# Routed FFN: norms, logits and choice made in the block endings of the attention ahead of it, and its lists in source order

## The chip, the core and the metric

The kernel runs on one core of one Trainium2 chip. TensorE (PE; its weight loads are PEld) multiplies matrices, VectorE (DVE) and ScalarE (ACT) work elementwise, GpSimd (POOL) issues the indirect DMAs, SyncE (SP) the plain ones. Each engine takes its instructions in order; semaphores order them against each other. The metric is the device time of one execution in microseconds (us), of which the median of several runs is taken. Lower is better.

## What is computed

The input is 6250 rows of 256 numbers, a graph of 206250 edges sorted by destination, and a second edge list of 131072 edges. Four layers each add to the rows `x`:

```
x = x + gnn0(layernorm(x))    # graph attention, 4 heads of 64
x = x + ffn0(layernorm(x))    # 8 experts, 2 for each row
x = x + gnn1(layernorm(x))    # weighted sum over edges, two products
x = x + ffn1(layernorm(x))    # graph attention as router, 4 experts
```

The change lies between the first two. `ffn0` is

```
logits = xt @ Wr + br                      # xt = layernorm(x)
probs  = softmax(logits); the 2 greatest of 8, divided by their sum, are the gates
for each expert e:  h = gelu(layernorm(xt) * ln_g[e] + ln_b[e] @ W1[e] + b1[e])
out    = sum over the chosen e of gate * (h @ W2[e] + b2[e])
```

(in the third line the norm with its scale and shift is taken first, then the product). So each row is normed twice: `xt` feeds the logits, its own norm feeds the experts.

## The kernel before

Rows lie in SBUF as `X`, 49 blocks of 128 rows. `fast` (L1778) runs these stages in turn.

**First attention** (`gat_stream`, L1146, called at L1863). The sorted edges are 1612 tiles of 128, taken in 202 pieces of eight. The loop over `s_` (L1352) is a software pipeline under `tc.manual_schedule()`, so each engine gets its instructions in the order of the source: step `s_` gathers piece `s_` from the table `tab` (POOL, L1214), loads what piece `s_+2` needs (SP), scores piece `s_-2` (`node_parts`, `scores`), every fourth step finds the greatest scores of a batch of 32 tiles and takes their exponentials (`turn_scores`, `greatest`, `turn_back`, whose ACT and DVE lines are L1285 and L1286), builds the one-hot matrices of piece `s_-6`, weights its messages (`messages`, L1293) and sums those of piece `s_-7` on PE (`sums`, L1316). A piece's tile `g` has nine buffers. The message weights `pe` lie in a PSUM tile of their own. When a block of 128 rows is complete, `done` (L1845) divides, adds the bias, applies relu and adds to `X[:, b, :]` (L1861).

**Front of the routed FFN** (`ffn0`, L652). For chunks of seven blocks it makes `xt`, the norm of `X` (`layernorm`, L247: bn_stats L252, bn_aggr L253, Sqrt on ACT L242, reciprocal L244, one tensor_scalar L256), then `xn`, the norm of `xt`, stores `xn` to the DRAM table `tab_x` (L671), transposes `xt` by PE, multiplies it with `wr` (L678) and adds `br` (L679). Then, for all 49 blocks at once, softmax, `top2` (the rank of each expert by pairwise comparison, L274 and L276) and gates.

**Lists** (first half of `routed_ffn`, L457). Expert parameters are gathered into `par` and stored as `par_d` (L478 to L483). A running count per expert gives every (row, choice) its place; 98 pairs of one-hot matrices `ro`, `qo` (L549, L551) and a product (L553) turn the places into the lists `gi` (which row to gather, L560) and `so` (where to put the result).

**Experts** (second half). 56 tiles of 256 places: SP loads the expert's weights by a register that it reads from `te`, POOL gathers `xg` from `tab_x`, PE transposes, multiplies (L601), ACT applies gelu, PE multiplies (L614), POOL scatters to `tab_y`. Then `X` gets the two results of each row (L632).

**What is drawn from `beside`.** `ffn0` takes a generator: `sorted_edges` (L1396) sorts the 131072 keys of the second edge list on chip (its compare stages are L1447 and L1448 on tile `A`; from the eleventh merge on it also transposes by PE), and `runs_of` (L1520) prepares lists for the third layer. Four steps of it are drawn after every expert tile:

```python
for _ in range(4):
    next(beside, None)
```

`ffn0` and `routed_ffn` are not under `tc.manual_schedule()`: a planner with a cost model orders their instructions, and it may set instructions of the generator well ahead of their place in the source, into gaps that it sees, also into the norms and the lists.

Of the kernel before, what the change touches and what calls it, by code (L numbers as in the profile page):

```python
# [20 lines left out]
F32 = mybir.dt.float32  # L21
# [50 lines left out]
def tile_kernel(ctx, tc, src_ins, out):  # L72
# [192 lines left out]

    def top2(pool, v, n_exp, nt=NT):

        rank = pool.tile([P, nt, n_exp], F32, name="rank")
        cmp = pool.tile([P, nt, n_exp], F32, name="cmp")
        nc.vector.memset(rank, 0.0)  # L270
        for j in range(n_exp):
            for a, b, op in ((0, j, OP.is_gt), (j + 1, n_exp, OP.is_ge)):
                if a < b:
                    nc.vector.tensor_tensor(cmp[:, :, a:b], v[:, :, j:j + 1].to_broadcast([P, nt, b - a]),  # L274
                                            v[:, :, a:b], op=op)
                    nc.vector.tensor_add(rank[:, :, a:b], rank[:, :, a:b], cmp[:, :, a:b])  # L276
        sel = pool.tile([P, nt, n_exp], F32, name="sel2")
        nc.vector.tensor_scalar(sel, rank, 1.5, None, op0=OP.is_lt)
        return sel

    def per_row(pool, op, a, n_exp, name):
        r = pool.tile([P, NT], F32, name=name)
        nc.vector.tensor_reduce(r, a, AX.X, op)
        return r[:, :, None].to_broadcast([P, NT, n_exp])

    def divide(pool, dst, a, by, n_exp, name):
        r = pool.tile([P, NT], F32, name=name)
        nc.vector.tensor_reduce(r, by, AX.X, OP.add)
        nc.vector.reciprocal(r, r)
        nc.vector.tensor_mul(dst, a, r[:, :, None].to_broadcast([P, NT, n_exp]))  # L290
# [166 lines left out]
    def routed_ffn(keep, tab_x, sel, gates, pre, beside):  # L457
# [12 lines left out]
        par_d = dram.tile([n_exp, P, NPAR], F32, name="par_d")  # L470
# [4 lines left out]
        with tc.tile_pool(name="rk", bufs=1) as p, tc.tile_pool(name="rkw", bufs=4) as wp, \  # L475
                tc.tile_pool(name="rk_ps", bufs=1, space=PSUM) as pp:
            par = p.tile([P, n_exp, NPAR], F32, name="par")
            with nc.allow_non_contiguous_dma(reason="biases along the partitions"):  # L478
                for o, n, v in ((0, FC, b1), (FC, KD, I[f"{pre}_ln_g"]), (FC + KD, KD, I[f"{pre}_ln_b"])):
                    pt = p.tile([P, n_exp, n], F32, name=f"par{o}")  # L480
                    nc.sync.dma_start(pt, v.rearrange("e (c p) -> p e c", p=P))
                    nc.vector.tensor_copy(par[:, :, o:o + n], pt)
                nc.sync.dma_start(par_d.rearrange("e p c -> p e c"), par)  # L483
# [168 lines left out]
    def ffn0(beside):  # L652

        E0 = I["L0_ffn_Wr"].shape[1]
        with tc.tile_pool(name="f0", bufs=1) as f0:
            gates = f0.tile([P, NT, E0], F32, name="gates")
            sel0 = f0.tile([P, NT, E0], F32, name="sel0")
            tab_x = dram.tile([NP, D], F32, name="tab_x")
            with tc.tile_pool(name="f0w", bufs=2) as lp, \
                    tc.tile_pool(name="f0_ps", bufs=2, space=PSUM) as pp:  # L660
                wr = lp.tile([P, KD, E0], F32, name="wr", bufs=1)
                nc.sync.dma_start(wr, I["L0_ffn_Wr"].rearrange("(k p) f -> p k f", p=P))
                br = lp.tile([P, E0], F32, name="br", bufs=1)
                nc.sync.dma_start(br, rows(I["L0_ffn_br"]))
                lo = lp.tile([P, NT, E0], F32, name="lo", bufs=1)
                for t0, n in chunks(NT, CH):
                    xt = lp.tile([P, CH, D], F32, name="xt")
                    layernorm(lp, xt, X[:, t0:t0 + n, :], n)
                    xn = lp.tile([P, CH, D], F32, name="xn")
                    layernorm(lp, xn, xt, n)  # L670
                    nc.sync.dma_start(tab_x[t0 * P:(t0 + n) * P].rearrange("(t p) d -> p t d", p=P),  # L671
                                      xn[:, :n])
                    for j in range(n):
                        xT = lp.tile([P, KD, P], F32, name="xT")
                        transposed(pp, xT, xt[:, j, :])
                        pr = pp.tile([P, E0], F32, name="pr")
                        for k in range(KD):
                            nc.tensor.matmul(pr, xT[:, k], wr[:, k], start=(k == 0), stop=(k == KD - 1))  # L678
                        nc.vector.tensor_add(lo[:, t0 + j, :], pr, br)  # L679
                nc.vector.tensor_sub(lo, lo, per_row(lp, OP.max, lo, E0, "mx"))  # L680
                nc.scalar.activation(lo, lo, AF.Exp)
                pb = lp.tile([P, NT, E0], F32, name="pb", bufs=1)
                divide(lp, pb, lo, lo, E0, "sm")
                sel = top2(lp, pb, E0)
                nc.vector.tensor_copy(sel0, sel)
                nc.vector.tensor_mul(pb, pb, sel)
                divide(lp, gates, pb, pb, E0, "sg")
            routed_ffn(f0, tab_x, sel0, gates, "L0_ffn", beside)
# [95 lines left out]
    def general():  # L784
        with ExitStack() as held1:
# [57 lines left out]
            ffn0(iter(()))  # L843
# [302 lines left out]
    def gat_stream(s, H, CD, si, il, dl, tab, NI, early, done, parts=1, beside=None):  # L1146
# [13 lines left out]
        with ExitStack() as st:  # L1160
            pool = lambda name, bufs, **k: st.enter_context(tc.tile_pool(name=f"{s.name}_{name}", bufs=bufs, **k))
            gp = pool("gs", 1)
            mp = pool("gw", 2)
            pp = pool("gp", 1, space=PSUM)
            nid = window_nodes(s, gp)
            NB = gp.tile([P, NT, 3, ND], BF, name="NB")
            nb_d = dram.tile([NP, 3 * ND], BF, name=f"{s.name}_nb") if s.group else None
            nbw, sums_of, ready, moved = {}, {}, [], []
            with tc.tile_pool(name="split", bufs=1) as sp:
                r = sp.tile([P, NT, ND], F32, name="r")  # L1170
                nc.vector.tensor_copy(NB[:, :, 0, :], NI)
                nc.vector.tensor_sub(r, NI, NB[:, :, 0, :])
                nc.vector.tensor_copy(NB[:, :, 1, :], r)
                nc.vector.tensor_sub(r, r, NB[:, :, 1, :])
                nc.vector.tensor_copy(NB[:, :, 2, :], r)
                if s.group:
                    nc.sync.dma_start(nb_d.rearrange("(t p) d -> p t d", p=P), NB.rearrange("p t s d -> p t (s d)"))
            ips = place_iota(pp)
# [96 lines left out]
            def turn_back(i, d, M):  # L1275
                pz = pp.tile([P, 3, P], F32, name="zt")
                nc.tensor.transpose(pz[:, 0], d, ident)
                nc.tensor.transpose(pz[:, 1], M[:, :P], ident)
                pb = pz[:, :2].rearrange("p k (t h) -> p k t h", h=H)
                pe = ps[i] = (pp if parts == 1 else gp).tile([P, B, H], F32, name="pe", bufs=1)  # L1280
                nc.scalar.activation(pe, pb[:, 0], AF.Exp)
                for q in range(i * PB, min((i + 1) * PB, npiece)):
                    t0, n = span(q)
                    o = t0 - i * B
                    nc.scalar.activation(piece[q][:, :n, DH:DH + H], pb[:, 0, o:o + n], AF.Exp)  # L1285
                    nc.vector.tensor_tensor(piece[q][:, :n, DH + H:], pb[:, 1, o:o + n],  # L1286
                                            il[:, t0:t0 + n, None].to_broadcast([P, n, H]), op=OP.mult)

            def messages(q):
# [3 lines left out]
                nc.vector.tensor_mul(gh, gh, ps[i][:, o:o + n, :, None].to_broadcast([P, n, H, CD]))  # L1293
# [30 lines left out]
            def keep_sums():  # L1324

                while ended:
                    i = ended.pop(0)
                    t = mp.tile([P, W], F32, name="kept", bufs=3)
                    nc.scalar.copy(t, acc.pop(i).rearrange("p s w -> p (s w)"))
                    moved.append((i, t))  # L1330
# [17 lines left out]
            with tc.manual_schedule():  # L1348
# [3 lines left out]
                for s_ in range(max(npiece + 7, PB * nbatch + 3) + 2):  # L1352
# [4 lines left out]
                    beside()  # L1357
                    k, q = s_ - 2, s_ - 7
# [21 lines left out]
                    if s.group:  # L1380
                        keep_sums()
                        while ready:
                            b = ready.pop(0)
                            done(b, sums_of.pop(b), items.pop(b), mp)
                    while ended:
                        b = ended.pop(0)
                        done(b, acc.pop(b), items.pop(b), mp)
# [390 lines left out]
    def fast(flag_s0, last_d, dl_d):  # L1778
# [7 lines left out]
        tab = dram.tile([NP, D + H0], F32, name="tab")  # L1786
        with tc.tile_pool(name="gat0f", bufs=1) as g0:
            si = g0.tile([P, C * P], I32, name="si")
            dl = g0.tile([P, C * P], F32, name="dl")
            il = g0.tile([P, C * P], F32, name="il")  # L1790
# [54 lines left out]
            def done(b, acc, hs, mp):  # L1845
# [15 lines left out]
                nc.vector.scalar_tensor_tensor(X[:, b, :], o, 0.0, X[:, b, :], op0=OP.max, op1=OP.add)  # L1861

            gat_stream(s0, H0, C0, si, il, dl, tab, NI, early, done)  # L1863


# [6 lines left out]
        with tc.tile_pool(name="sort", bufs=1) as sp, tc.tile_pool(name="sort_ps", bufs=1, space=PSUM) as pp:  # L1872
# [4 lines left out]
            ffn0(itertools.chain(sorted_edges(s1, sp, pp, si1, dl1, il1, flag1),  # L1877
                                 runs_of(s0, sp, pp, si_d, wab_d, dab_d)))
# [239 lines left out]
```

## Time and profile before

| | us |
|---|---|
| median of 10 runs | 6606.87 (6602.35 to 6609.58) |
| the profiled execution | 6605.38 |
| its span | 6603.6 |
| first gather of the attention | 174.3 |
| last row of `X` from the attention written | 2249.1 |
| norms and logits | 2249.1 to 2374 |
| choice | 2374.4 to 2395.2 |
| lists | 2395.2 to 2461.9 |
| first expert product | 2474.6 |
| last expert product | 3325 |
| combination into `X` | 3325 to 3395 |
| weighted sum of the third layer | 3436 to 5495 |

Times in the profile are from the start of the span. Line numbers (L1214) are those of the kernel before. A group's row gives line, engine, operation, tiles, shape and count, then busy us, mean ns of one, then the idle time of the engine just before them with what ended it. A row of the timeline gives start, length, engine and instruction.

### The profile page before, as it was taken

How to read it: one execution, taken by the hardware profiler on the slowest of the kernel's cores; microseconds unless marked ns; L12 is line 12 of the kernel's file. 1: busy time of each engine (PE TensorE's matmuls, PEld its weight loads, DVE VectorE, ACT ScalarE, POOL GpSimd, SP SyncE). 2: the span in 40 equal slices, each digit the busy share in tenths (PEclk: the TensorE clock that was granted, in tenths of full speed). 3: DMA queues.
4: the chain of work that ended last, by engine and by line, in shares of the span. 5: the costliest groups of instructions: out<-in, count | busy, mean ns of one | idle time of the engine just before them, and what ended most of it. 6: DMA issues, size and time to landing. Idle time of an engine off the chain costs nothing.

```text
span 6603.6 us, 62175 instructions
## 1 busy us (share of the span) xinstructions
PE 3866.5 (59%) x17463; PEld 2941.9 (45%) x17463; DVE 4398.5 (67%) x10540; ACT 1008.7 (15%) x2527; POOL 4095.6 (62%) x4320
## 2 busy tenths in 40 slices
PE   4466666666666659999913566666666667111111
PEld 3344444444444448888712344444444445111111
DVE  5455555555555683345267888888888883888888
ACT  2000000000000102222300122222222223000000
POOL 0777777777777302233217777777777775777774
PEclk9677777777777669999955777887888788555555
DMA  4555555555555216556553444444444443233332
GB/s 134 139 139 137 137 140 138 137 139 137 138 139 138 73 50 205 184 192 218 179 188 107 115 118 123 122 122 118 123 122 122 118 122 75 61 68 68 68 69 53
DMA packets 495558, 821.80 MB, mean 124 GB/s; under 512 B 142672, under 2 KB 314915, under 8 KB 495170
## 3 DMA queue, kind: packets, MB, share of 16 engines
q0 software_dynamic: 190880, 462.26, 26.8%
q1 hardware_dynamic: 291654, 343.79, 17.3%
q10 hardware_dynamic: 12668, 11.68, 0.6%
q8 instruction: 141, 2.31, 0.1%
q14 instruction: 215, 1.76, 0.1%
HBM read 743.27 MB, written 77.29 MB: 124 GB/s over the span
## 4 chain that ended last, share of the span: by engine, by line
POOL 33%; PE 17%; issue 17%; DVE 16%; DMA 15%; ACT 1%; ACTq 0%; DVEq 0%; SPq 0%; another core or an unknown queue 0%; POOLq 0%
POOL g L234 17%; POOL g L1214 16%; DMA g<-tab,si 7%; PE ph L601 5%; PE py L614 5%; DMA g<-tab_ef,si 3%; PE acc L1316 3%; DMA g<-tab_1f,si1s 2%; DVE X L1756 2%; DVE run L1921 2%; DVE g L1293 1%; DVE oh L1107 1%; PE ph L1830 1%; DVE ot L1224 1%; DVE z L1246 1%
## 5 line engine op out<-in xcount | busy, mean ns | idle before, releaser
L234 POOL DMA_INDIRECT g<-tab_ef,si x1616 | 1532.9, 949 | 602.6 <-issue 574.0
L1214 POOL DMA_INDIRECT g<-tab,si x1612 | 1538.9, 955 | 494.5 <-issue 411.6
L1921 DVE SCALAR_TENSOR_TENSOR run<-g,wab,run 128x256 f32<-128x256 f32 x2626 | 1263.9, 488 | 339.9 <-DMA g<-tab_ef,si 264.3
L1316 PE MATMUL acc<-g,oh 128*128 128x264 f32 x3224 | 1052.5, 492 | 336.2 <-DVE g L1293 331.1
L1316 PEld LDWEIGHTS acc<-g,oh 128*128 128x128 f32 x3224 | 780.4, 250 | 559.5 <-DVE g L1293 389.5
L1214 POOL DMA_INDIRECT g<-tab_1f,si1s x787 | 769.9, 978 | 251.6 <-issue 212.1
L2035 PE MATMUL acc<-run,oh 128*128 128x256 f32 x808 | 319.4, 535 | 708.7 <-DVE oh L1925 705.7
L2035 PEld LDWEIGHTS acc<-run,oh 128*128 128x128 f32 x808 | 199.3, 264 | 818.1 <-issue 442.0
L1246 DVE TENSOR_TENSOR z<-g,nd 128x32 f32<-128x32 f32 (+1 forms) x301 | 58.0, 193 | 707.2 <-DMA g<-tab,si 644.9
L1293 DVE TENSOR_TENSOR g<-g,pe 128x2048 f32<-128x2048 f32 (+2 forms) x301 | 487.1, 1618 | 0.0
L1657 PE MATMUL pf<-xt,w 128*128 128x512 f32 (+1 forms) x832 | 416.8, 636 | 102.7 <-ACT h L1662 95.9
L1668 PE MATMUL pf<-w,h 128*128 128x256 f32 x1568 | 405.4, 409 | 71.3 <-ACT y L1673 60.7
L1316 PE MATMUL acc<-s,oh 128*128 128x72 bf16 x1267 | 96.4, 251 | 594.4 <-DVE s L1298 594.4
L601 PE MATMUL ph<-xe,w 128*128 128x256 f32 x1792 | 405.6, 383 | 4.5 <-DVE xe L589 4.5
L614 PE MATMUL py<-w,h 128*128 128x256 f32 x1792 | 398.7, 380 | 0.0
L1668 PEld LDWEIGHTS pf<-w,h 128*128 128x128 f32 x1568 | 317.5, 207 | 132.6 <-ACT y L1673 68.4
L577 POOL DMA_INDIRECT xg<-tab_x,gi x112 | 123.4, 1102 | 402.6 <-PE pt L586 317.2
L601 PEld LDWEIGHTS ph<-xe,w 128*128 128x128 f32 x1792 | 341.7, 193 | 50.7 <-DVE xe L589 4.9
L1316 PEld LDWEIGHTS <-oh 128*128 128x128 bf16 x1267 | 89.9, 133 | 598.5 <-issue 495.5
L614 PEld LDWEIGHTS py<-w,h 128*128 128x128 f32 x1792 | 336.6, 191 | 43.1
L617 POOL DMA_INDIRECT tab_y<-y,so x112 | 119.0, 1062 | 276.1 <-DVE y L616 271.5
L1235 PEld LDWEIGHTS <-ot 128*128 128x128 bf16 x2879 | 116.0, 101 | 389.9 <-DVE ot L1224 347.6
(494 smaller groups left out, 5751.1 us busy)
## 6 DMA issues: line engine op xcount, KB each, us to landing
w<-in_L_ffn_W SPq DMA_DIRECT2D x112, 1024.0 KB
db<-s_d SPq DMA_DIRECT2D x299, 256.0 KB
g<-tab_ef,si POOLq DMA_INDIRECT x1616
g<-tab,si POOLq DMA_INDIRECT x1612
y_d<-y SPq DMA_DIRECT2D x196, 128.0 KB
yb<-y_d SPq DMA_DIRECT2D x49, 512.0 KB
g<-tab_1f,si1s POOLq DMA_INDIRECT x787
yy<-tab_y SPq DMA_DIRECT2D x7, 1792.0 KB
```

The costliest lines, as they stand in the source:

```text
L234: nc.gpsimd.indirect_dma_start(out=dst, out_offset=None, in_=table, in_offset=bass.IndirectOffsetOnAxis(ap=si[:, t:t + 1], axis=0))
L601: nc.tensor.matmul(ph, w1[:, k, f * P:(f + 1) * P], xe[:, k, :], start=(k == 0), stop=(k == KD - 1))
L614: nc.tensor.matmul(py, hs[f][:, i * P:(i + 1) * P], w2[:, f, :], start=(f == 0), stop=(f == FC - 1))
L1214: nc.gpsimd.indirect_dma_start(out=g[:, j, :DH + H], out_offset=None, in_=tab, in_offset=bass.IndirectOffsetOnAxis(ap=si[:, t0 + j:t0 + j ...
L1246: nc.vector.tensor_add(z[:, :n], g[:, :n, DH:DH + H], nd[:, :n, :H])
L1293: nc.vector.tensor_mul(gh, gh, ps[i][:, o:o + n, :, None].to_broadcast([P, n, H, CD]))
L1316: nc.tensor.matmul(acc[b].rearrange("p s w -> p (s w)"), oh[:, t - a], m_, start=(t == lo), stop=(t == hi))
L1657: nc.tensor.matmul(ph[:, :n], w1[:, e, k, f * P:(f + 1) * P], xts[g][:, k, :n], start=(k == 0), stop=(k == KD - 1))
L1668: nc.tensor.matmul(py[:, :D], hs[g, e, f][:, j * P:(j + 1) * P], w2[:, e, f, :], start=(f == 0), stop=(f == FC - 1))
L1756: nc.vector.scalar_tensor_tensor(X[:, b, :], v[:, e, :], gates[:, j, e:e + 1], X[:, b, :], op0=OP.mult, op1=OP.add)
L1921: nc.vector.scalar_tensor_tensor(at[:, i] if j < Q - 1 else r[i], g[:, j, :], w, at[:, i], op0=OP.mult, op1=OP.add)
L2035: nc.tensor.matmul(acc[i], oh[:, k], r[k], start=(q % 2 == 0 and k == 0), stop=(last and k == 1))
```

## The change

1. A class `Head` holds `lo` (logits), `sel`, `gates`, `wr`, `br`, `tab_x` and `par_d`. It is made before the attention and lives until the experts are done.
2. The attention's `done` ends with `spread` (bn_stats, bn_aggr, Sqrt) and returns a next step. `gat_stream` collects such steps with `follow` and runs each in the next round of its loop, between the loads and the scores: `normed` (norm of the block, statistics of the result), `twice` (two PE transposes, one ACT copy), `logits` (second norm, store of 128 rows to `tab_x`, product with `wr`, ACT copy). After blocks 21, 43 and 48 `chosen` follows: bias, softmax, ranks and gates for the blocks since the last one (22, 22, 5), one step of the generator `select` per round. The loop runs on until no step is left.
3. `expert_params` is drawn as the attention's `beside`: its three loads are issued in the first round, copies and store come 20 draws later (five draws a round).
4. The PSUM tile of `pe` is replaced by one tile `mix` of 512 columns: `pe` in the first 128, the transposes in the next 256, the logits in eight more.
5. To make room, `il` is bf16, `kept` has two buffers for three, and the split of node values `NB` lies in the short-lived pool `split`; the pools of the pipeline open after that pool has closed.
6. The list part of `routed_ffn` comes under `tc.manual_schedule()`: its instructions run in source order, and the planner puts none of the generator's among them. The experts' part is as before, with the same generator.

The core of the diff, and the new functions:

```diff
-    def routed_ffn(keep, tab_x, sel, gates, pre, beside):
+    def expert_params(p, par_d, pre):
+        b1, g, b = (I[f"{pre}_{s}"] for s in ("b1", "ln_g", "ln_b"))
...
+            for o, n, v in ((0, FC, b1), (FC, KD, g), (FC + KD, KD, b)):
+                pt = p.tile([P, n_exp, n], F32, name=f"par{o}")
+                nc.sync.dma_start(pt, v.rearrange("e (c p) -> p e c", p=P))
+                parts.append((o, n, pt))
+            for _ in range(20):
+                yield
+            for o, n, pt in parts:
+                nc.vector.tensor_copy(par[:, :, o:o + n], pt)
+            nc.sync.dma_start(par_d.rearrange("e p c -> p e c"), par)
+    def routed_ffn(keep, tab_x, sel, gates, par_d, pre, beside):
...
-                tc.tile_pool(name="rk_ps", bufs=1, space=PSUM) as pp:
+                tc.tile_pool(name="rk_ps", bufs=1, space=PSUM) as pp, tc.manual_schedule():
...
+    def select(pool, tag, lo, br, sel, gates, n, n_exp):
+        wide = [P, n, n_exp]
+        nc.vector.tensor_add(lo, lo, br[:, None, :].to_broadcast(wide))
+        nc.vector.tensor_sub(lo, lo, per_row(pool, OP.max, lo, n, n_exp, f"mx{tag}"))
+        nc.scalar.activation(lo, lo, AF.Exp)
+        yield
+        divide(pool, gates, lo, lo, n, n_exp, f"sm{tag}")
+        yield
+        yield from ranks(sel, lo, gates, n_exp)
+        nc.vector.tensor_scalar(sel, sel, 1.5, None, op0=OP.is_lt)
+        nc.vector.tensor_mul(gates, gates, sel)
+        divide(pool, gates, gates, gates, n, n_exp, f"sg{tag}")
...
-            mp = pool("gw", 2)
-            pp = pool("gp", 1, space=PSUM)
...
-            NB = gp.tile([P, NT, 3, ND], BF, name="NB")
...
             with tc.tile_pool(name="split", bufs=1) as sp:
+                NB = (sp if s.group else gp).tile([P, NT, 3, ND], BF, name="NB")
...
+            mp = pool("gw", 2)
+            pp = pool("gp", 1, space=PSUM)
...
-                pe = ps[i] = (pp if parts == 1 else gp).tile([P, B, H], F32, name="pe", bufs=1)
-                nc.scalar.activation(pe, pb[:, 0], AF.Exp)
+                if i == 0:
+                    ps[0] = gp.tile([P, B, H], F32, name="pe") if pe is None else pe
+                nc.scalar.activation(ps[0], pb[:, 0], AF.Exp)
...
-                for s_ in range(max(npiece + 7, PB * nbatch + 3) + 2):
+                last, s_, later = max(npiece + 7, PB * nbatch + 3) + 1, -1, []
...
+                while s_ < last or later:
+                    s_ += 1
...
                     beside()
+                    now, later[:] = list(later), []
+                    for f, a in now:
+                        follow(f(*a))
...
+                return normed, (b, mp) + spread(mp, X[:, b, :])
+            def spread(mp, x):
+                bs = mp.tile([P, 6], F32, name="bs", bufs=3)
+                nc.vector.bn_stats(bs, x)
+                mv = mp.tile([P, 2], F32, name="mv", bufs=6)
+                nc.vector.bn_aggr(mv, bs)
+                sd = mp.tile([P, 1], F32, name="sd", bufs=6)
+                nc.scalar.activation(sd, mv[:, 1:2], AF.Sqrt, bias=eps)
+                return mv, sd
+            def scaled(mp, xl, x, mv, sd):
+                rs = mp.tile([P, 1], F32, name="rs")
+                nc.vector.reciprocal(rs, sd)
+                nc.vector.tensor_scalar(xl, x, mv[:, 0:1], rs, op0=OP.subtract, op1=OP.mult)
+            def normed(b, mp, mv, sd):
+                xt = mp.tile([P, D], F32, name="xt", bufs=3)
+                scaled(mp, xt, X[:, b, :], mv, sd)
+                return twice, (b, mp, xt) + spread(mp, xt)
+            def twice(b, mp, xt, mv, sd):
+                pt = mix[:, P:P + D].rearrange("p (k e) -> p k e", k=KD)
+                for k in range(KD):
+                    nc.tensor.transpose(pt[:, k], xt[:, k * P:(k + 1) * P], ident)
+                xT = mp.tile([P, KD, P], F32, name="xT")
+                nc.scalar.copy(xT, pt)
+                return logits, (b, mp, xt, mv, sd, xT)
+            def logits(b, mp, xt, mv, sd, xT):
+                scaled(mp, xt, xt, mv, sd)
+                nc.sync.dma_start(head.tab_x[b * P:(b + 1) * P], xt)
+                head.logits(mix[:, P + D:P + D + E0], xT, b)
+                if b in ends:
+                    t0 = max([e + 1 for e in ends if e < b], default=0)
+                    return chosen, (head.select(hp, t0, b + 1 - t0),)
+            def chosen(parts):
+                for _ in parts:
+                    return chosen, (parts,)
+            ends = (NT // 2 - 3, NT - 6, NT - 1)
...
+                mix = xp.tile([P, 4 * P], F32, name="mix")
+                par = head.params(hp)
+                gat_stream(s0, H0, C0, si, il, dl, tab, NI, early, done, beside=lambda: next(par, True) is None,
+                           pe=mix[:, :P].rearrange("p (b h) -> p b h", h=H0))
...
-            ffn0(itertools.chain(sorted_edges(s1, sp, pp, si1, dl1, il1, flag1),
-                                 runs_of(s0, sp, pp, si_d, wab_d, dab_d)))
+            head.ffn(f0, itertools.chain(sorted_edges(s1, sp, pp, si1, dl1, il1, flag1),
+                                         runs_of(s0, sp, pp, si_d, wab_d, dab_d)))
+        chosen_by.close()
```

## The prediction

> **What bounds the kernel now.** I read the page's chain first, then busy time by stage, then the timeline around the stage that is changed.
>
> ```profile
> POOL g L234 17%; POOL g L1214 16%; DMA g<-tab,si 7%; PE ph L601 5%; PE py L614 5%; DMA g<-tab_ef,si 3%; PE acc L1316 3%; DMA g<-tab_1f,si1s 2%; DVE X L1756 2%; DVE run L1921 2%; DVE g L1293 1%; DVE oh L1107 1%; PE ph L1830 1%; DVE ot L1224 1%; DVE z L1246 1%
> ...
> L1214 POOL DMA_INDIRECT g<-tab,si x1612 | 1538.9, 955 | 494.5 <-issue 411.6
> ```
>
> The first attention is L1214: 1612 gathers on POOL, 0.955 us each and 0.30 us of issue between them, 2033 us from 174 to 2207. The list of waits has no POOL wait there over 0.3 us but one of 3.1: POOL never waits for a buffer. I matched gathers with the sums that free their buffers: from the end of the sums of a piece to the gather that takes its buffer nine pieces later at least 20.3 us pass, with a piece every 10.09 us. So this stage has room on every engine but POOL.
>
> ```profile
> 1400.00:2000.00 600.00, 387.40 (x1634) 287.36 (x1632) 346.29 (x619) 32.39 (x148) 454.86 (x477) 0.75 0.51 139
> 2000.00:2249.00 249.00, 159.70 (x673) 120.20 (x671) 148.37 (x264) 15.00 (x66) 156.94 (x166) 0.78 0.42 113
> 2249.00:2374.00 125.00, 66.97 (x294) 58.64 (x294) 101.53 (x408) 24.29 (x65) 4.69 (x55) 0.50 0.16 53
> 2374.00:2467.00 93.00, 44.56 (x200) 31.79 (x200) 85.65 (x310) 0.53 (x1) 3.62 (x7) 0.72 0.15 23
> 2467.00:2700.00 233.00, 226.66 (x1069) 197.94 (x1070) 69.96 (x129) 63.08 (x131) 67.47 (x65) 0.97 0.63 207
> ```
>
> Columns: stretch, length, busy us of PE, PEld, DVE, ACT, POOL, then granted clock, DMA share, GB/s. In the attention DVE is busy 58% and ACT 5%. From 2249 to 2467, norms and logits, then choice and lists, DVE is busy 86% and POOL next to nothing: a serial stretch on DVE. Then the experts, with PE full.
>
> ```profile
> 2248.64 0.43 DVE L1861 SCALAR_TENSOR_TENSOR X<-o,X 128x256 f32<-128x256 f32 x1
> ...
> 2374.39 0.55 DVE L283 TENSOR_REDUCE mx<-lo 128x49 f32<-128x392 f32 x1
> ...
> 2395.20 1.35 DVE L486 TENSOR_TENSOR_SCAN inc<-sel 128x49 f32<-128x49 f32 x8
> ...
> 2403.09 0.20 DVE L482 COPY par<-par 128x64 f32<-128x64 f32 x1 [5.23 <-DMA par<-in_L_ffn_b]
> ...
> 2461.67 0.21 DVE L560 TENSOR_SCALAR gi<-gi 128x112 int32<-128x112 int32 x1
> ...
> 2474.55 9.77 PE L601 MATMUL ph<-xe,w 128*128 128x256 f32 x32
> ```
>
> This is the ruler: last row of X at 2249.07; choice from 2374.4; lists 2395.20 to 2461.88; first expert product 12.7 us later. From X to gi: 212.8 us, all on the path.
>
> **The change, term by term.** The 212.8 us fall away; five terms take their place.
>
> (a) In the attention, per block, DVE gets two bn_stats, two aggregates, two reciprocals, two 128x256 tensor_scalars. The same four shapes run in the weighted sum: 0.427 (L1984), 0.182 (L1986), 0.155 (L1993), 0.41 (L1995, its least): 2.4 us. PE gets two transposes and four logit passes, 1.5 us at half clock; ACT two Sqrt, two copies and up to four table loads of 1.28; SP one 128 KB store. A block ends every 41 us; in that time DVE waits 13.2 us for gathers to land (644.9 us over 49 blocks), so 2.4 us of work and some 5 us of waits fit. The steps `normed`, `twice`, `logits` each come one iteration later than their inputs, so little queues behind them. The select of 22 blocks is 4 small instructions, about 1 us, an iteration. The weighted sum shows the cover holding: there the same chain runs beside 1604 gathers with DVE 82% busy, and POOL waits 0.3 us at a time. What remains is POOL's own time. The 44 gathers there that overlap an L1995 average 0.966 us against 0.946 without neighbours, and in the attention those beside an L1198 store to the queue 0.99: 98 x 0.02 + 49 x 0.04, some **3 us** (0 to 14; the latter if each of the 98 costs the 0.14 by which the slowest common gathers, 1.087, exceed 0.946).
>
> The new tile `mix` puts `pe`, the transposes and the logits into one PSUM tile. How such sharing behaves is seen at L1285 and L1286: ACT and DVE read different parts of one `zt` and strictly alternate, each idle 0.26 us until the other ends. So the transposes wait for the message product (2.28 us) of the iteration before. PE stands there with `node_parts` behind it, DVE's `nd` behind that; about 1.2 us twice per block, inside the 20.3 us.
>
> (b) The drain, 2207 to 2249, has no POOL cover; DVE, PE and ACT alternate. Into it fall the endings of blocks 46 and 47 (DVE 2.4 and 1.8 us, PE 1.5 and 0.55), three steps of the second select (3 us), and two table loads back to Exp (2.6): 11.9 us, of which a little lies in existing waits: **10 us** (4 if only the loads and half of PE's part show, 20 with six hand-overs at `mix` at 1.2 us on top).
>
> (c) Block 48 has everything bare: statistics 0.6, table load and Sqrt 1.6, reciprocal and scaling 0.6, statistics and Sqrt 0.9, copy, logits, copy 1.6, hand-overs 0.3; then the select of 5 blocks: 3 small DVE instructions, table load, Exp, 3 more, 2.5; 28 rank instructions at 0.16 (L274 and L276 of the last stage, 0.160 and 0.169), 4.6; the last five 0.85. That is **14 us** (9 with loads hidden and pairs overlapping, 20 with every hand-over at 0.26).
>
> ACT's loads have a rule against them. In this trace the instruction behind each ACT_TABLE_LOAD starts 0.01 us after its 1.28. The Trainium skill ("ScalarE: Activation LUTs", What ACT_TABLE_LOAD costs) adds a drain of about 1.38 us to each load. By that rule four loads on the path in (b) and (c) would make the sum 5.5 us longer; the trace disagrees.
>
> (d) Lists, now in source order without the sort: 66.7 us less 10 sort compares ahead of the ro/qo loop (0.62 each from start to start, 6.2), 0.5 for two behind it, 6.4 for the wait on `par` and its copies, is 53.6. Filling is lost too: dependents start some 0.04 us after their input ends, independents 0.09 before; 25 instructions x 0.13 = 3.3. **57 us** (53 to 63). The loop itself, 98 x 0.445 = 43.6 us, is untouched.
>
> (e) The experts start 12.7 us behind gi as before. The sort's start, 11.4 us of preparation and 51 compares, moves here: 46 us of DVE. Its first 55 stages take 81 us in all; a tile of 14.25 us leaves DVE over 12 free, so they end by tile 7; the next step, which needs PE, ran at 2690.6, tile 15. So PE should not see it. POOL's 4.7 us of iotas and memsets and 1 MB of keys come here too: **2 us** (0 to 8).
>
> The moves of `par`, `wr` and `br` to the start cost nothing beside nine free buffers: `par` took 8.3 us to land, and POOL has 90 us before it needs a buffer back. SP is held 7.4 us issuing `par`, with the loads of two pieces ahead behind it, again under 20.3.
>
> Sum: 212.8 - (3 + 10 + 14 + 57 + 2) = 126.8. The profiled execution took 6605.4 us (span 6603.6), giving 6478.6; the median of the runs is 1.5 us higher, so **6480 us**. With the terms' ends the case runs from 6460 to 6519, where all bad ends meet.
>
> **Rivals.**
>
> 1. The pools move: g, db and the rest now open behind the closed `split`, which also holds `NB`. If g takes NB's place, the first gather (174.28) waits until NB is stored (issued 176.11, read from 189.77): 15.5 us later, all of it on POOL: 6495. For: POOL is the bound. Against: db is asked for first and is larger (6 KB against 3.9), and a late db costs 1.5 us of a slack of 20. 12%.
>
> 2. DVE's scalings hold POOL off: 98 x 0.41 us, 0.76 of it on a gather in work, 31 us: 6511. Against: the 0.966 above. The Trainium skill ("SBUF — State Buffer", SBUF: two separate sides) states that POOL can't write DMA descriptors while DVE runs a two-port instruction. 6%.
>
> 3. The experts give the sort back: 46 us, if the stages run at their places, 4 a tile, and PE stands before the transposes of the sort. It does stand later: of 150 us from 3099 PE is busy 132.7. 6526. 7%.
>
> 4. **Slower**: the block endings make DVE, not POOL, the bound of the attention, through the shared `mix`. It decides where a block's added work and waits exceed 13.2 us plus 126.8/49 = 15.8. I count 7.4; if hand-overs cost a whole iteration's alternation, 18 us say, it is 6480 + 49 x (18 - 13.2) = 6715. The 20.3 us help only once. 8%, a quarter of that near no change.
>
> 5. More gain: the 17 us of PE stalls just named depend on where the planner puts the sort; without them 6463, with light ends under 6455. 5%.
>
> **Numbers.** The forecast has 62%. The range 6455 to 6532 takes in the forecast and rivals 1 to 3. About 0.2% is what a measurement of this kernel can tell from no change: faster 0.92, same 0.02, slower 0.06.
>
> **What the profile would show.** (a) L1214 near 0.957 us, a piece still every 10.1 us, last gather near 2210; a gap over 0.3 us would speak for rival 4, a first gather near 190 for rival 1. (b, c) Last X near 2262, the last gates near 2276. (d) No A<-A compare between the scans and gi; gi near 2333. (e) First expert product near 2346, its 56 tiles still ending some 850 us later. I am wrong if pieces take over 10.3 us or the experts' stage grows by tens of us.

## The result, and the profile after

The changed kernel takes 6493.1 us (median of 8 runs, 6488.3 to 6496.6) against 6606.8 for the kernel before (28 runs): ratio 0.983, 95% interval 0.982 to 0.984. The forecast was 6480, the gain 113.7 us for 126.8 forecast. The span of the profiled execution fell from 6603.6 to 6486.6 us, by 117.0; the execution profiled after lies 4.7 us under the median of its runs.

The ruler of the prediction, in the timeline of the kernel after (start, length, engine, line):

```profile
187.90 1.10 POOL L1260 DMA_INDIRECT g<-tab,si  x1 [14.50 <-DMA s_nb<-NB]
...
2272.93 0.42 DVE L1921 SCALAR_TENSOR_TENSOR X<-o,X 128x256 f32<-128x256 f32 x1
...
2285.35 0.25 DVE L515 TENSOR_TENSOR_SCAN inc<-sel 128x49 f32<-128x49 f32 x1
...
2355.23 0.21 DVE L589 TENSOR_SCALAR gi<-gi 128x112 int32<-128x112 int32 x1
...
2366.46 3.78 PE L630 MATMUL ph<-xe,w 128*128 128x256 f32 x8 [0.64 <-DVE xe L618]
```

From X's last row to `gi` there are now 82 us instead of 213. But the first gather starts 13.6 us later, held by a DMA, the store of `NB`. Cut at these marks, the two spans compare so:

| stretch | before | after | difference |
|---|---|---|---|
| start to first gather | 174.3 | 187.9 | +13.6 |
| first to last gather | 2033.0 | 2036.7 | +3.7 |
| last gather to last row of X | 41.8 | 48.7 | +6.9 |
| last row of X to `gi` | 212.8 | 82.1 | -130.7 |
| `gi` to first expert product | 12.7 | 11.0 | -1.6 |
| the experts' products | 849.0 | 841.1 | -7.8 |
| the rest | 3280.1 | 3279.0 | -1.0 |

The stages by window (columns as in the prediction's windows):

```profile
1400.00:2000.00 600.00, 365.35 (x1682) 282.96 (x1681) 378.49 (x741) 84.24 (x236) 455.21 (x475) 0.76 0.52 141
2000.00:2273.00 273.00, 175.86 (x773) 134.60 (x772) 182.41 (x375) 44.16 (x115) 170.61 (x178) 0.81 0.43 115
2273.00:2285.00 12.00, 1.68 (x6) 1.21 (x6) 8.42 (x49) 2.58 (x7) 1.53 (x4) 0.50 0.07 22
2285.00:2355.00 70.00, 44.57 (x200) 31.27 (x200) 68.97 (x272) 0.00 (x0) 3.72 (x54) 0.79 0.05 16
```

In 600 us of the attention DVE does 32 us more and ACT 52 more, and POOL's 455 stand unchanged: the work went beside the gathers. Two groups of the profile's page (the second is VectorE's first instruction on the gathered rows, so what it waits for is the gathers) say what it used up:

```profile
L1260 POOL DMA_INDIRECT g<-tab,si x1612 | 1545.5, 959 | 505.7 <-issue 426.0
...
L1292 DVE TENSOR_TENSOR z<-g,nd 128x32 f32<-128x32 f32 (+1 forms) x301 | 58.0, 193 | 477.7 <-DMA g<-tab,si 419.6
```

A gather takes 0.959 us for 0.955 before, and no gap between two of them is over 0.32 us. VectorE's wait for gathers to land fell from 644.9 to 419.6 us: 4.6 us a block are spent, some 8.5 are left.

Seven of the runs below (e5 to e10, e12) fell on chips on which the kernel before takes 7802 to 7897 us, for a reason that stays open, and in their profiles POOL waits up to 16.8 us between two gathers; it does not pace the attention there, so of these runs single instructions are read, and times only beside each other.

### The profile page after: what moved, and what is told of

Same layout as the page of the kernel before. It is cut to its first block, busy times and chain, and to the rows that moved or that the text cites. A ratio compares the mean times of both kernels' runs of the same rounds, so it can differ in the third digit from the quotient of the medians.

```text
span 6486.6 us, 62324 instructions
## 1 busy us (share of the span) xinstructions
PE 3787.6 (58%) x17463; PEld 2900.3 (45%) x17463; DVE 4446.4 (69%) x10655; ACT 1161.7 (18%) x2758; POOL 4102.8 (63%) x4320
## 4 chain that ended last, share of the span: by engine, by line
POOL 23%; PE 13%; issue 11%; DVE 11%; DMA 6%; ACT 0%; ACTq 0%; DVEq 0%; another core or an unknown queue 0%; POOLq 0%; SPq 0%
POOL g L234 18%; PE ph L630 6%; PE py L643 5%; POOL g L1260 5%; DMA g<-tab_ef,si 3%; DMA g<-tab_1f,si1s 2%; DVE X L1813 2%; DVE run L2028 2%; DVE oh L1152 1%; DMA yy<-tab_y 0%; DVE ot L1270 0%; DVE qo L580 0%; PE pf L1714 0%; DVE X L661 0%; PE pt L615 0%
## 5 line engine op out<-in xcount | busy, mean ns | idle before, releaser
L1260 POOL DMA_INDIRECT g<-tab,si x1612 | 1545.5, 959 | 505.7 <-issue 426.0
L1363 PE MATMUL acc<-g,oh 128*128 128x264 f32 x3224 | 995.8, 472 | 225.0 <-DVE g L1340 220.3
L1363 PEld LDWEIGHTS acc<-g,oh 128*128 128x128 f32 x3224 | 754.5, 240 | 412.7 <-DVE g L1340 250.3
L1340 DVE TENSOR_TENSOR g<-g,mix 128x2048 f32<-128x2048 f32 x202 | 457.6, 2265 | 0.0
L1292 DVE TENSOR_TENSOR z<-g,nd 128x32 f32<-128x32 f32 (+1 forms) x301 | 58.0, 193 | 477.7 <-DMA g<-tab,si 419.6
L633 ACT ACTIVATE h<-ph,pa 128x256 f32<-128x256 f32 x448 | 212.3, 474 | 437.6 <-PE ph L630 436.7
```

The source lines that it names most:

```text
L633: nc.scalar.activation(h, ph, AF.Gelu, bias=pa[:, f:f + 1])
L1260: nc.gpsimd.indirect_dma_start(out=g[:, j, :DH + H], out_offset=None, in_=tab, in_offset=bass.IndirectOffsetOnAxis(ap=si[:, t0 + j:t0 + j ...
L1340: nc.vector.tensor_mul(gh, gh, ps[0][:, o:o + n, :, None].to_broadcast([P, n, H, CD]))
L1363: nc.tensor.matmul(acc[b].rearrange("p s w -> p (s w)"), oh[:, t - a], m_, start=(t == lo), stop=(t == hi))
```

## The experiments

**e1, the pool's buffers wait tile by tile.** This asks what holds the first gather.

```diff
-            mp = pool("gw", 2)
+            mp = pool("gw", 2, reuse_waits="tile")
```

> The changed kernel, but the pipeline's pool waits tile by tile for the memory of the pool that closed ahead of it, not for the whole of it. Theory A (rival 1 of the prediction, by way of the pool and not of one buffer's place: the first gather waits for the store of NB): first gather back near 174.5 from 187.9, all that follows 13 us earlier, 6493 becomes 6480. Theory B (the late start comes from the new loads at the front or from the nodes' own store): first gather stays at 187 to 190, 6493.

Measured: 6484.9 us (6476.6 to 6490.9), ratio to before 0.9815 (0.9802 to 0.9828). Its timeline at the start:

```profile
173.22 0.59 POOL L1182 IOTA s_nid<- 128x1 f32 x5 [104.10 <-DMA tab<-tb]
...
174.26 1.10 POOL L1260 DMA_INDIRECT g<-tab,si  x1 [0.45 <-POOL s_nid L1182]
```

The gather no longer waits for the store, only for POOL's own iota, and starts where it did before. So it was the reuse of the closed pool's memory that held it, and g's first buffer did not itself lie on `NB`: with waits counted tile by tile it had nothing to wait for. (One later gather, at 187.55, waits 0.6 us more than the others, put to a DMA.) The medians give back 8.2 of the 13.6 us. In the two profiled executions the first gather gains all 13.6, and the experts' products, which the edit does not touch, take 4.1 us more.

**e2, the lists without the manual order.**

```diff
-                tc.tile_pool(name="rk_ps", bufs=1, space=PSUM) as pp, tc.manual_schedule():
+                tc.tile_pool(name="rk_ps", bufs=1, space=PSUM) as pp:
```

> The changed kernel with the list part left to the planner (no manual order). Theory A (the manual order binds only the lists against each other and the planner puts the sort among them either way): lists from the first scan to gi 65 to 73 us as against 70.1, total 6490 to 6498. Theory B (the manual order keeps work out that the planner would put in): lists 78 us or more, 6501 or more.

Measured: 6487.2 us (6482.5 to 6493.0), ratio 0.9817 (0.9803 to 0.9830). From the first scan to `gi` 60.9 us instead of 70.1, shorter than either theory had it. The planner put instructions of the sort among the lists too, but 19 on VectorE where the kernel after has 33. So the order by hand kept nothing out; it cost some 9 us in this stage, 6 in the medians, whose ranges overlap.

**e3, the sort's buffers asked for behind the lists,** so that none of its instructions can stand among them.

```diff
-        with tc.tile_pool(name="sort", bufs=1) as sp, tc.tile_pool(name="sort_ps", bufs=1, space=PSUM) as pp:
...
-            head.ffn(f0, itertools.chain(sorted_edges(...), runs_of(...)))
+        def behind(st):
+            sp = st.enter_context(tc.tile_pool(name="sort", bufs=1))
+            pp = st.enter_context(tc.tile_pool(name="sort_ps", bufs=1, space=PSUM))
+            return itertools.chain(sorted_edges(...), runs_of(...))
+        head.ffn(f0, behind)
```

In `routed_ffn`, `behind` is called after the lists' pools have closed and ahead of the pool `ff`.

> The changed kernel, but the pools of the sort open only when the lists' pool has closed, so that no instruction of the sort can run before the lists end. Theory A (term d of the prediction failed only because the sort's first part still stood among the lists, and the copy of cnt waited for POOL's memsets): scan to gi 70.1 becomes 55 to 58, the copy of cnt 2.26 becomes 0.2, the experts' 841 us unchanged, 6479. Theory B (what the lists get the experts give back): lists the same 55 to 58, but the experts 12 to 16 us longer, 6493. Theory C (source order itself costs the 13 us by exposed latencies): lists stay at 68 to 70.

Measured: 6478.9 us (6473.9 to 6481.5), ratio 0.9806 (0.9792 to 0.9819). The lists of the kernel after, and what stands among them:

```profile
2286.69 2.54 POOL L1165 MEMSET base<- 128x24 f32 x49
...
2287.00 2.26 DVE L518 COPY cnt<-inc 128x8 f32<-128x8 f32 x1
...
2300.61 1.22 DVE L1487 TENSOR_TENSOR B<-B,B 128x1024 f32<-128x1024 f32 x1
...
2304.49 1.22 DVE L1490 TENSOR_TENSOR A<-A,A 128x1024 int32<-128x1024 int32 x1
...
2307.26 0.69 DVE L1504 TENSOR_TENSOR A<-A 128x512 f32<-128x512 f32 x1
```

and of this run:

```profile
2283.07 0.17 DVE L518 COPY cnt<-inc 128x8 f32<-128x8 f32 x1
...
2339.21 0.22 DVE L589 TENSOR_SCALAR gi<-gi 128x112 int32<-128x112 int32 x1
```

L1473 to L1505 are the sort's preparation and first compares. The account of the change says that the planner puts none of the generator's instructions among the lists. The trace shows otherwise: the manual order keeps the listed instructions in order among themselves, and 33 of the sort's on VectorE stand between them. Without them the lists take 58.0 us (2281.4 to 2339.4), 12.1 less; 2.1 of this is the copy L518, which here does not stand beside POOL's memsets. The experts' products take 846.3 us with the sort all inside them (842.5 in e11 below), and with a head start 841.1 in the kernel after, 845.2 in e1 and 846.0 in e2: a cost to PE of the sort's later start does not show beside this spread.

A second gain shows besides: from `gi` to the first product 7.2 us instead of 11.0. SyncE's waits between the scans and the first product say why (line, what it waited for, us, times, longest); the kernel after, and e3:

```profile
SPq L597 <- DVE gi L588: 61.1, 1, 61.1
SPq L593 <- DVE te L542: 5.6, 1, 5.6
```

```profile
SPq L597 <- DVE te L542: 9.5, 1, 9.5
```

The reading of the first expert's number from `te` is L593 in the kernel after and, four lines further down, L597 in e3. Behind it comes the first load, `pa`, L597 in the kernel after: it waits 61.1 us for the lists' end, which it does not read, and is issued at 2354.86; the weights then land together with the gathered rows. In e3 there is no such wait, `pa` is issued at 2287.72, and the weights land beside the lists. The kernel before has such a wait too (52.1 us at its L568), so this gain is not one that the change had lost. That the pool `ff` takes over the lists' memory in the one and not in the other is inferred.

**e4, `pe` in SBUF as a tile of its own,** the sharing of `mix` undone for it.

```diff
-                gat_stream(s0, H0, C0, si, il, dl, tab, NI, early, done, beside=lambda: next(par, True) is None,
-                           pe=mix[:, :P].rearrange("p (b h) -> p b h", h=H0))
+                gat_stream(s0, H0, C0, si, il, dl, tab, NI, early, done, beside=lambda: next(par, True) is None)
```

> The changed kernel with the message weights pe in SBUF, so that the PSUM tile mix holds only the transposes and logits of the block endings. Theory A (POOL bounds the attention and the shared tile costs at most a few hand-overs in the drain): pieces stay at 10.1 us, last gather to last X 48.8 becomes 45 to 48, total 6489 to 6493. Theory B (sharing the tile is what the block endings cost): drain back to 42 to 43, 6486 or less. Theory C (a message product with both inputs in SBUF is dearer for POOL): gathers above 0.97 us, 6510 or more.

Measured: 6850.1 us (6845.4 to 6853.1), ratio 1.0365 (1.0351 to 1.0379): 357 us slower than the kernel after. This is theory C, which named only a floor of 6510. From the last gather to the last row of X 48.0 us pass, for 48.7 with the shared tile: the sharing shows no cost in the drain beside the 48.2 to 49.0 of e1 to e3, and theory B is out. The page's row of the gathers, and the timeline around one message product (L1340), of this run:

```profile
L1260 POOL DMA_INDIRECT g<-tab,si x1612 | 1896.7, 1177 | 504.8 <-issue 414.7
```

```profile
1011.82 0.95 POOL L1260 DMA_INDIRECT g<-tab,si  x1 [0.30 <-ACT g L1332]
1012.77 2.28 DVE L1340 TENSOR_TENSOR g<-g,pe 128x2048 f32<-128x2048 f32 x1
1013.07 2.79 POOL L1260 DMA_INDIRECT g<-tab,si  x1 [0.30 <-issue]
```

and around one of the kernel after:

```profile
1017.14 2.28 DVE L1340 TENSOR_TENSOR g<-g,mix 128x2048 f32<-128x2048 f32 x1
1017.83 0.94 POOL L1260 DMA_INDIRECT g<-tab,si  x1 [0.30 <-issue]
1019.08 0.95 POOL L1260 DMA_INDIRECT g<-tab,si  x1 [0.31 <-issue]
```

The product takes 2.28 us in both. With both operands in SBUF the gather that starts beside it takes 2.79 us, and ends 0.81 us after the product; with one operand in PSUM it takes 0.94. In the whole trace 196 gathers start while such a product runs. Each of them ends 0.82 us after its product, they take 2.74 us on the mean, and what they take over 0.946 us adds up to 352 us. The 76 gathers that were running already when a product began take 0.947. All 1612 gathers together take 351 us longer (1896.7 against 1545.5), of the 357 us lost. So `pe` in PSUM, where it lies before and after, is worth more than the change itself.

**e5 and e6, twelve more 128x256 adds in each block ending,** to see whether this holds for short instructions, and whether VectorE has room.

```diff
                 nc.vector.tensor_add(o, o, acc[:, :D])
+                for _ in range(12):
+                    nc.vector.tensor_add(o, o, acc[:, :D])
```

and `bias` in place of `acc[:, :D]` in e6.

> The changed kernel with 12 more 128x256 tensor_adds in each block ending of the first attention, one operand of each in PSUM (the block's sums), so its attention output is altered. 12 x 0.46 = 5.5 us of VectorE a block, under the 8.5 us a block for which VectorE still waits for gathers there (417.6 us over 49). Theory A (room on VectorE, POOL paces): the gathers' stage stays 2037 us, L1260 stays near 0.959 us; only the two or three endings after the last gather show, +11 to +16 us, so some 6506. Theory B (VectorE or its hand-overs already pace the blocks): +49 x 5.5 = 270 us, 6763. Theory C (any VectorE instruction on SBUF holds POOL off): gathers beside the adds are longer, stage +20 us or more.

> The same 12 tensor_adds a block with both operands in SBUF (the bias row in place of the sums); the output is altered likewise. VectorE's time is the same 5.5 us a block. Theory A (POOL is held off while VectorE reads two operands from SBUF, as in the run with pe in SBUF): gathers that lie beside the adds are longer. In the changed kernel a gather beside one of the three such instructions takes 1.04 to 1.07 instead of 0.947; 4.4 gathers a block at +0.1 give +22 us above the run with PSUM operands; if POOL gets no turn between two adds it is up to the whole 5.5 us a block, +270 us. Theory B (no holding off): the same time as the run with PSUM operands.

Measured: 7875.2 and 7859.3 us, before on that chip 7897.1; with POOL not the bound, the times decide nothing. The gathers do (e5, then e6):

```profile
1520.92 5.43 DVE L1920 TENSOR_TENSOR o<-o,bacc 128x256 f32<-128x256 f32 x12
1521.96 0.95 POOL L1260 DMA_INDIRECT g<-tab,si  x1 [0.30 <-issue]
1523.21 0.95 POOL L1260 DMA_INDIRECT g<-tab,si  x1 [0.30 <-issue]
```

```profile
1517.86 5.48 DVE L1920 TENSOR_TENSOR o<-o,bias 128x256 f32<-128x256 f32 x12
1518.74 0.94 POOL L1260 DMA_INDIRECT g<-tab,si  x1 [0.30 <-issue]
1519.98 0.95 POOL L1260 DMA_INDIRECT g<-tab,si  x1 [0.30 <-issue]
1521.24 1.08 POOL L1260 DMA_INDIRECT g<-tab,si  x1 [0.30 <-DVE o L1920]
1522.63 1.07 POOL L1260 DMA_INDIRECT g<-tab,si  x1 [0.30 <-issue]
```

Over the whole trace, gathers that lie beside these adds and no other VectorE instruction take 0.945 us in e5 (135 of them, all within 0.94 to 0.96) and 1.036 in e6 (133 of them). In e6 not every one is longer: 30 take under 0.98, and most of the rest 1.06 to 1.10. POOL does get its turn between two short adds. On all gathers it is 0.954 against 0.966, 20 us, near the +22 of theory A.

**e8 and e10, `pe` in SBUF (the edit of e4) and the product in eight instructions.**

```diff
-                nc.vector.tensor_mul(gh, gh, ps[0][:, o:o + n, :, None].to_broadcast([P, n, H, CD]))
+                for j in range(n):
+                    nc.vector.tensor_mul(gh[:, j], gh[:, j], ps[0][:, o + j, :, None].to_broadcast([P, H, CD]))
```

> The kernel with pe in SBUF (6850 us), the message product of 128x2048 made as eight of 128x256: the same elements, VectorE some 1.2 us a piece longer. Theory A (a gather's start waits for the end of the VectorE instruction that reads both operands from SBUF, so the length of one instruction sets the cost): a wait of at most 0.42 us, two or three gathers a piece at +0.1 to +0.2, so +60 to +110 us above the changed kernel, 6555 to 6605, no gather near 3 us. Theory B (POOL is held off for all of the product's time, whatever its pieces): as before or worse, 6850 to 7100.

> The message product with pe in SBUF in eight instructions of 128x256, once more, where POOL paces the gathers. In the run before this one a gather that lay beside nothing but such an eighth took 1.033 us against 0.946 beside nothing, and 0.980 on the mean of all 1612. Theory A (a gather waits for the end of one instruction at most): POOL's gathers take 1612 x (0.980 - 0.959) = 35 us more than in the changed kernel, which gives some 6528 (6515 to 6560), against 6850 with the product in one instruction. Theory B (VectorE's 1.2 us more a piece, 5 us a block of the 8.5 left, brings other waits with it): over 6600.

Measured: 7826.5 and 7841.9 us (before there 7897.1 and 7874.7). Gathers beside nothing but such an eighth take 1.033 and 1.032 us, all 1612 on the mean 0.980 and 0.979, for 1.177 with the product in one instruction. By the gathers' own time that is 35 and 33 us over the kernel after instead of 351, and under the 60 to 110 of theory A; the whole time where POOL paces stays unmeasured.

**e7 and e12, thirty adds,** 13.8 us a block, for the point at which VectorE becomes the bound.

> As the first of these runs with 30 adds a block, 13.8 us, where 8.5 us of VectorE's waits for gathers are left; the output is altered. Theory A (the room is what VectorE waits for gathers): 5.3 us a block too much, VectorE becomes the bound: POOL shows gaps over 0.31 us, stage +49 x 5.3 = 260, with three endings behind the last gather at 13.8 each some 6790. Theory B (other waits, those of 204.7 us for ScalarE among them, give way too): the stage hardly grows and the time is some 6535.

> The 30 extra adds a block with one operand in PSUM once more, where POOL paces the gathers (the block's output is altered). They take 30 x 0.46 = 13.8 us of VectorE a block; 8.5 us of its waits for gathers are left. Theory A (the room is what VectorE waits for gathers, as the prediction's fourth rival counts): 5.3 us a block too much, gaps between POOL's gathers, stage 2037 + 260, and the endings behind the last gather 13.8 us each, some 6790. Theory B (other waits of VectorE, 204.7 us for ScalarE among them, give way too): the stage hardly grows, and only the two or three endings behind the last gather show, some 6530.

Measured: 8102.1 and 8066.3 us, before on the two chips 7897.1 and 7801.8. Eighteen more adds than e5 (18 x 0.46 x 49 = 406 us of VectorE) lengthen the stage of the gathers by 197 us (2640 in e7 against 2443, on one chip). VectorE does cost time there, but on a chip on which POOL is not the bound; where rival 4 begins stays open.

**e9 and e11, the edits of e1 and e3 together.**

> The changed kernel with two edits together: the attention's working pool waits for the former users of its memory tile by tile (alone 6484.9), and the sort's buffers are asked for behind the lists, so that the sort starts with the experts (alone 6478.9). Theory A (the two act in different places and their gains add): 13.6 us at the first gather and 12.1 us between the scans and gi against the changed kernel, so some 6467 (6462 to 6475). Theory B (the sort, started later, costs the experts what the lists gain): some 6480.

> The two edits together once more (working pool waiting tile by tile, sort's buffers behind the lists), where POOL paces the gathers as in the first four runs. Theory A (the gains add): some 6467 (6462 to 6475) beside a kernel before of 6607; first gather near 174.3, scans to gi 58, experts 846. Theory B (the sort, started later, costs the experts what the lists gain): some 6480.

Measured: e9 7783.5 us (before 7874.7, ratio 0.9874, 0.9847 to 0.9901); e11 **6460.8 us** (6460.1 to 6464.5; before 6604.2, ratio 0.9784, 0.9771 to 0.9797). That is 32 us under the kernel after. First gather 175.5, lists 58.0, `gi` to the first product 7.3, products 842.5: the gains add. e9 has the same stages at the start and in the lists (173.6, 58.0), but decides nothing on the time. The sum expected was 6467. Of the 6 us below it, 3.8 are the shorter way from `gi` to the first product, which that sum left out; the rest is not placed.

## Why the prediction held, and where it was off

The mechanism was right: a serial stretch goes, and what replaces it hides behind POOL. Of the signs named ahead, those for this held: a piece still comes every 10.1 us, no gap between gathers is over 0.32, and the experts did not grow. Two spoke against single terms: the first gather at 187.9, and compares of the sort between the scans and `gi`. By terms:

- **(a) 3 us (0 to 14): 3.7.** As written the term's own sum, 98 x 0.02 + 49 x 0.04, gives 3.9. The gathers themselves take 6.5 us more (1612 x 0.004), less 2.8 of gaps, as one of 3.1 near the second piece is gone. 43 gathers beside the second scaling (L1937) average 1.006 us, some 2.6 us in all; the rest is spread. The room was counted on the safe side: 4.6 us a block used of 13.2, for 7.4 counted. One part of it was sized too small: at `mix` PE waits for the message product 5.0 us a block (176.1 us before the transposes, 70.6 before the logits), for 2.4 counted. This cost nothing that shows, as it stays far under the 20.3 us.
- **(b) 10 us: 6.9. (c) 14 us: 12.0.** Both within their ends. The table loads there take 1.28 us each. Behind four of the seven the next ACT instruction starts 0.01 us later, so the trace shows no drain on top; the other three wait for the block's statistics. The prediction's "each" was too wide in the same way: in the kernel before it holds for 82 of 147 loads, and behind the other 65 ACT waits for PE or VectorE.
- **(d) 57 us (53 to 63): 70.1, the term that failed.** The step that failed is "in source order without the sort": the sort did not leave. Its 33 instructions on VectorE and the copy held beside POOL's memsets cost the 12 us that e3 takes away; without them the lists take 58.0, for 57 worked out. I took a statement of the code for a fact of the schedule.
- **(e) 2 us (0 to 8): -9.5** for the way from `gi` and the products, outside its ends. Of the products' -7.8 at least a part is chance, perhaps all: the same experts took 842.5 to 848.6 us in e1 to e4 and e11, 0.4 to 6.5 us under the 849.0 of the one execution before. That the sort stays off PE's path was right: no head start is needed (e3, e11).
- **Left out of the sum: +13.6.** Rival 1, at 12%, came true at nearly its price of 15.5. The argument against it asked whether g's memory is NB's. It need not be: with the pool's waits taken as a whole, any tile of the pool waits for everything that lay there. The chance was too low, since the pool's move was in the diff and POOL is the bound.

The misses are +13.6 and +13.1 on one side and -11.5, -3.1, -2.0 on the other, with +0.7 and -1.0 for (a) and the rest: together +9.8, the 126.8 forecast less 117.0 of span. That the time came within 13 us of the forecast is in part luck: two misses of 13 us were more than half met by three the other way. So is that 6493 lies beside the 6495 of rival 1, since (d) missed as well.

**Rival 2**, VectorE holding POOL off, is a true mechanism that this change hardly meets: the scalings cost a few us, not 31. Gathers beside the first scaling average 0.949 us, beside the second 1.006, and why two instructions of one shape differ stays open. What e4 and e6 show is the hold by instructions with two operands in SBUF, not by the scalings, which have one. The Trainium skill ("SBUF — State Buffer", SBUF: two separate sides) describes an exclusive lock on a port pair that VectorE and POOL share, held for the whole instruction. The 2.79 us beside a 2.28 us product, and 1.03 beside one eighth of it, agree with that. **Rival 3** is excluded by e3; **rival 4** did not come at 4.6 us a block, and its threshold is open. **Rival 5** is not shown: PE's stalls within the experts went from 18.2 to 14.5 us (14.3 to 16.2 in e1, e2, e3 and e11), but they are 18.1 in e4, whose experts are unchanged.

## What to carry to other kernels

When work moves behind the bound engine, follow that engine's first instruction too: a pool opened where another has just closed can make it wait for the closed pool's last DMA (13.6 us here). That code is written in order, or under a manual order, does not keep a planner from putting other work among it; opening the other work's buffers later does. Where gathers on POOL are the bound, leave one operand of every long VectorE tensor_tensor in PSUM, or cut the instruction into short ones; of the second way only the gathers' own time is measured here.

## What the runs showed of the hardware

- A tensor_tensor with both operands in SBUF holds back an indirect gather that starts while it runs: in e4 the 196 such gathers end 0.82 us after the product's end and take 2.74 us on the mean and 3.06 at most, for 0.947 beside nothing. A gather that was already running is not held (76 of them, 0.947). With one operand in PSUM there is no hold: 0.946 for the 388 gathers that start within the product in the kernel after. For 0.42 us instructions it is 0.09 us a gather (e6).
- It seems to go the other way too: in the kernel after a 128x8 copy in SBUF (0.17 us in e3) stood 2.26 us while 49 memsets ran on POOL (2.54 us). The memsets ended at 2289.23, the copy at 2289.26. In e3, where the memsets fall elsewhere, a 128x1024 tensor_scalar in SBUF stood 2.08 us beside them, for 0.68 where it runs alone in the kernel after:

```profile
2348.47 1.77 POOL L1169 MEMSET base<- 128x16 f32 x32
2348.96 2.08 DVE L1487 TENSOR_SCALAR A<-B 128x1024 int32<-128x1024 f32 x1
```

One-column tensor_scalars beside 17 of the memsets in e3 take 0.15 us and are not held, so not every instruction is. No run was made for this; the matching ends are the evidence.
